# A four-layer graph network: the last add moved to GpSimd, and the planner's constants and rank offsets set anew

## The chip, the cores and the metric

The kernel runs on one core of a Trainium2 chip. The metric is the device time of one execution in microseconds; the lower the better. The core has a matmul engine (TensorE, "PE" in the profile), a vector engine (VectorE, "DVE"), an activation engine (ScalarE, "ACT"), GpSimd ("POOL"), and SyncE ("SP"), which here does nothing but issue DMA transfers.

## The reference, cut to what matters

The input is `x`, 128 graphs of 128 nodes with 256 features, and `adj`, a 128x128 matrix of zeros and ones for each graph. Four layers follow each other; each normalizes `x`, applies relu, and adds the result of a graph layer to `x`.

```python
A = (adj != 0)
# layer 0: three steps of a gated recurrent cell
h = relu(layernorm(x)); h0 = h
for i in range(3):
    m = h @ weight[i]
    aggr = einsum('bst,bsd->btd', A, m)
    h = gru_cell(aggr, h)        # r, z, n from aggr @ w_ih.T and h @ w_hh.T
x = x + h
# layer 1: sums over neighbours, by relation (adj holds only 0 and 1 here)
h = relu(layernorm(x)); x = x + (einsum(adj == 1, h) @ w1 + b1)
# layers 2 and 3: attention over neighbours
h = relu(layernorm(x)); Wh = h @ W.T
e = leaky_relu(Wh @ a1 + (Wh @ a2).T); e = where(adj, e, -inf)
x = x + softmax(e) @ Wh
```

The change touches the line `x = x + h` of layer 0, and the order in which everything is issued.

## The kernel before, in words

The 128 graphs are worked on in 32 groups of four (`G = 4`), so one tile has 128 partitions and 4 x 128 = 512 columns. Up to five groups are open at once (`AHEAD = 5`), in different layers. For the gates and for two of the layers' weights an operand is split into three parts in a rounded format (`F32R`): `forms` writes `hi` (L955 on ACT or L957 on DVE), `lo` (L961 on DVE) and their difference (L470, on POOL in nearly all cases), and PE makes three passes for each product (L992).

**One group.** `load` brings `x` and `adj`. `norm` computes the statistics on DVE (L696 and the small instructions up to L720), the power -0.5 on POOL (L722), and the scaled relu on ACT (L743). The recurrent cell runs three times in `step`: gathers over the neighbours (L974), the products of the gates (L992), gate functions on ACT (L1005, L1013, L1023, L1040) and DVE (L1035, L1042, L1045, L1048). The state is kept with features in the partitions. To come back to nodes in the partitions it is transposed by `turn`: DVE transposes 32x32 blocks inside a tile (L490), a transfer writes the tile to DRAM (`give`, L493, `swap<-big`), and four transfers read it back with the blocks exchanged (`take`, L502, `big<-swap`, or `wide<-swap` for the two tiles at a group's start, which are taken together). After the third step the two halves of `h` so transposed are added to `x` by `residual` (L1080), one instruction of 128x512 for each half; `x` is fetched a second time for this (`x1_`, L513). In the last two groups PE transposes instead and DVE adds straight from PSUM (L1073). Then come layer 1 (`neighbours`, with `bias` on POOL at L756) and two attention layers (`attention`, `attend`; L1119 computes two dot products per graph on DVE). The matmul of a layer with its neighbours is L765, with its weights L819 or L775. The attention's rows go through DRAM as well (`line<-small`, `big<-line`).

**The order.** Nothing is issued in program order. Every piece of work is recorded as an `Op` with its engine or engines, its planned length, what it reads and writes, and a `late` for the time from its end until its result may be read by another engine. `Plan.order` then simulates the engines with these planned times and writes out one order for all of them; each engine executes its own part of it strictly in sequence and waits by semaphores. The rank of an operation is its group times `PERIOD` (`CLOSE` for the last groups), minus the length of the longest way from it to its group's end, plus an offset from the table `OFFSETS`, which has an entry for each stage and each place in the code. The stages stand three times in the table: 0 to 7 for most groups, 10 to 17 for the last four, 20 to 27 for the first. On each engine the operation of lowest rank among those that can start is placed; an operation that could start only over `NEAR` ns later stands back. `SOON` is the margin by which an operation with two possible engines goes to its second.

**Planned times of transfers.** An operation on SP has the issue time as its length (`dma`, 470 ns; four times that for a `take`), and its result may be read by an engine `e` after `late + LAG["SP"] + HOP[e]`, that is `late` + 4500 + 40 ns for DVE or ACT, or after `late + OWN["SP"]` by another transfer of SP. `late` is `GIVE`, `TAKE`, `LINE` or `SPREAD` for the transfers of `turn` and `attend`, and 0 for the others. So a `take` has 4 x 470 + 2040 ns in the plan before.

**The add in question.** It is recorded with two engines, `(dve(T), 1250)` ns on DVE and POOL, and `port=True`: the plan lets no two operations with that mark run at the same time on DVE and POOL.

A branch on the largest entry of `adj` chooses between two programs; with these inputs the one described here runs.

Of the kernel before, what the change touches and what calls it, by code (L numbers as in the profile page):

```python
# [18 lines left out]
P = 128  # L19
# [19 lines left out]
OWN = {"PE": 0, "ACT": 125, "DVE": 125, "POOL": 80, "SP": 2500, "ACTQ": 2500}  # L39
PERIOD = 29902  # L40
CLOSE = 7183
CLOSING = 2
SOON = -210
# [3 lines left out]
LINE, SPREAD = 0, -1000  # L47
GIVE = -400
TAKE = -2500
TENSOR = ()  # L50
BLOCK = 32
NEAR = 69
# [24 lines left out]
def act(n, ptrs=0):  # L77
    return 50 + 95 * ptrs + 0.833 * n


def dve(n):
    return 68 + n / 0.96


def dma(kb):
    return 470
# [3 lines left out]
    0: (-70252, -12514, 2287, 8809, -26238, -146194, 10750, 55634, 30994, -54821, -2879, -215, -254,),  # L90
    1: (-77596, -18751, -40109, -33244, -13055, -53723, -68528, 1773, -34806, -135119, 879, -98768, 51856,
        44795, -64452, -2716,),
    2: (-95804, -20611, 70568, -66959, -6282, -38365, 6331, 7167, -87557, -120685, 144159, 0, -60172, 22200,
        253, 2907, 38047,),
    3: (-102445, -23990, 38859, 16506, -38395, -77755, 61821, 576, 58832, 37279, 38392, 48590, -137270, -161,
        -4329, 88294, -5659, -1511, -24936, -35483,),
    4: (9420, 6970, 96990, 45577, 14137, -3081, -28597, -108133, -850, -77398, -8748, -81, 24213, -39147,
        5274, -117520, -39070, 4328, 73461, 2677, -9322, 38218,),
    5: (-53063, -10484, 13614, 9709, -9223, 0, 86360, -49387, 3891, -79089, 22834, -12125, 42, -143071,
        -20815, -7001, 39402, 8197, 210921, 979, -8129, 55104, -109511, 178418, -171023, -17919, -45955,  # L100
        32785, 202299, 15929, -75290, -16189,),
    6: (-8401, 1876, 0, -2867, -17545, -54409, -177384, 6635, -4173, 16809, 64025, 1422, -41374, 3498, 7298,
        112681, -960, 0, -167733, 3047, -20901, 48681, -50794, 104147, -14530,),
    7: (2011, -43268, -7473, -2193, -13120, 17374, 10030, 24727, -8835, -59753, 29500, -32772, -10542,
        -85496, -6214, -47593, 4322, -5746, -43839, -101654, -3101, 9392, -18883,),
    10: (31340, 140410, 166041, 86764, 86271, -82403, 47762, 173067, 157481, -33091, 90840, -8460, 85813,),
    11: (-90811, -5747, -11338, -10756, 2168, -27498, -36330, -9110, 13623, -65824, 59954, -36485, 65854,
        102114, -39462, 10659,),
    12: (-88894, -2718, 120398, -47746, 16864, -33143, 17060, 25017, -58235, -111482, 170409, 89873, -65258,
        61044, 3422, 23111, 49690,),  # L110
    13: (-59071, 17894, 109447, 41927, -4268, -51312, 111328, 77067, 108356, 88471, 46360, 263340, -35253,
        23414, 79162, 211888, 10834, -10383, 74698, 67176,),
    14: (-32758, 12684, 122607, -43352, -20519, -34186, -56784, -88737, -18648, -122741, -24236, -29303,
        31876, -49287, -17477, -128202, -71886, 71670, 64769, 11212, -103569, -34527,),
    15: (-186417, -106904, -40789, -64266, -8033, -13445, 16411, -115394, -129609, -221523, -34547, -153159,
        -40482, -146129, -99541, -93701, -50044, 14115, 99121, -155460, -34394, 49772, -135635, 90451,
        -238640, -50117, -75732, -67304, 110359, -120923, -153053, -106347,),
    16: (90192, 31519, 28924, 59971, 13927, -108659, -126696, 35607, 7022, 44259, 134646, 83504, 72967,
        -71833, 139898, 214088, -4475, 66727, -178916, 46932, 84371, 67621, 13000, 119832, 93548,),
    17: (2011, -43268, -7473, -2193, -13120, 17374, 10030, 24727, -8835, -59753, 29500, -32772, -10542,  # L120
        -85496, -6214, -47593, 4322, -5746, -43839, -101654, -3101, 9392, -18883,),
    20: (-107741, -75380, -118420, -44708, -69924, -229335, -95079, 10513, -7484, 27055, -96949, -215, -254,),
    21: (-241039, -37443, -85617, -204164, -130954, -212658, -180409, -165567, -39823, -261311, -133885,
        -103620, -20641, -66103, -225402, -138454,),
    22: (-120431, -90137, 129948, -127092, 11177, -90000, -80347, -35815, -106293, -139261, 141530, -54256,
        -129233, 7860, -119111, 29072, 3576,),
    23: (-144176, -87227, -85789, 1378, -81324, -238467, -3162, -78700, 46997, -3871, 33809, 42358, -177604,
        -35904, -119077, -63937, -38348, -135903, -24936, -35483,),
    24: (-200969, -199448, -70412, -199813, -160146, -250664, -235592, -342997, -205357, -303708, -186137,
        -202706, -168399, -243146, -236370, -300082, -270699, -214705, -104544, 2677, -9322, 38218,),  # L130
    25: (-61251, -50204, -55609, -84828, -90010, 10545, -51986, -177143, -111208, -144284, 59013, -46623,
        -56779, -179794, -83802, -190091, -64080, -63359, 54466, -41363, -72589, -54011, -140205, 135055,
        -306980, -77123, -140787, 32785, 202299, 15929, -75290, -16189,),
    26: (-81589, -13318, 8156, -109205, -83353, -110277, -231535, -35494, -89897, 10694, 20288, -77730,
        -166910, -72981, -43136, 895, -48027, -102602, -242066, -114463, -91143, 43689, -72571, 104147,
        -14530,),
    27: (2011, -43268, -7473, -2193, -13120, 17374, 10030, 24727, -8835, -59753, 29500, -32772, -10542,
        -85496, -6214, -47593, 4322, -5746, -43839, -101654, -3101, 9392, -18883,),
# [235 lines left out]
def kernel(  # L374
# [49 lines left out]
    def build(general):  # L424
# [53 lines left out]
        def turn(nm, srcs, dst=None, w=None):  # L478
# [7 lines left out]
            for k, (src, r) in enumerate(srcs):  # L486
                part = chunk(f"part{nm}{k}")

                def within(src=src, part=part):
                    nc.vector.transpose(part.t, src())  # L490

                def give(k=k, part=part):
                    nc.sync.dma_start(out=swap.t[k * G : (k + 1) * G].rearrange("g p c -> p g c"),  # L493
                                      in_=part.t.rearrange("p (g c) -> p g c", g=G))

                op("DVE", dve(T) + 15, within, r=[r], w=[part])
                op("SP", 470, give, r=[part], w=[(swap, {k})], late=GIVE)

# [6 lines left out]
            op("SP", 470 * P // BLOCK, take, r=[swap], w=[w], late=TAKE)  # L505
# [3 lines left out]

        def fetch(gi, name, after=()):  # L510
            xt = Buf(xs, f"{name}{gi}")
            for g2 in range(G // 2):
                op("SP", dma(256), lambda g2=g2: nc.sync.dma_start(  # L513
                    out=xt.t[:, 2 * g2 : 2 * g2 + 2, :],
                    in_=x[ds(gi * G + 2 * g2, 2)].rearrange("g n d -> n g d")),
                   w=[(xt, {2 * g2, 2 * g2 + 1})], after=after)
            return xt
# [4 lines left out]
        def again(gi, after):  # L522
            ai = Buf(adjs, f"again{gi}")
            op("SP", dma(256), lambda: nc.sync.dma_start(
                out=ai.t.rearrange("p (g j) -> p g j", g=G),
                in_=adj[ds(gi * G, G)].rearrange("g i j -> i g j")), w=[ai], after=after)
            return ai

        def load(gi):
            xt, ai = fetch(gi, "x0_"), Buf(adjs, f"adj{gi}")  # L530
            op("SP", dma(256), lambda: nc.sync.dma_start(
                out=ai.t.rearrange("p (g j) -> p g j", g=G),
                in_=adj[ds(gi * G, G)].rearrange("g i j -> i g j")), w=[ai])
            state[gi] = xt, ai
# [383 lines left out]
        def group(gi):  # L918
# [21 lines left out]
            def step(i, hs, hT):  # L940
# [136 lines left out]
                for k, h in enumerate(hs_new if i == L - 1 else ()):  # L1077
                    def residual(eng, k=k, h=h):
                        part = xt.t[:, :, k * P : (k + 1) * P]
                        (nc.gpsimd if eng == "POOL" else nc.vector).tensor_tensor(  # L1080
                            part, part, h.t.rearrange("p (g d) -> p g d", g=G), ALU.add)

                    op(("DVE", "POOL"), (dve(T), 1250), residual, r=[h], w=[(xt, set(range(G)))], port=True)
# [3 lines left out]
            for i in range(L):  # L1087
# [7 lines left out]
            op("SP", dma(256), lambda: nc.sync.dma_start(  # L1095
                out=aiT.t.rearrange("p (g j) -> p g j", g=G),
                in_=adjT[ds(gi * G, G)].rearrange("g i j -> i g j")), w=[aiT], after=late)
# [12 lines left out]
            def attention(i, mask):  # L1110
# [4 lines left out]
                for g in range(G):  # L1115
# [9 lines left out]
                    op("DVE", 850, terms, r=[(hs[g // 2], {g}), ub[i]], w=[junk, (s, {("ei", g)})], port=True)  # L1125
# [159 lines left out]
```

## Time and profile before

| what | us |
|---|---|
| median of 3 runs | 2353.08 |
| lowest and highest run | 2349.69, 2353.46 |
| profiled execution | 2353.06 |
| its span in the profile | 2351.2 |
| PE busy | 2291.9 (97%) |
| DVE busy | 1978.2 (84%) |
| ACT busy | 1582.0 (67%) |
| POOL busy | 912.4 (39%) |
| L1080 on DVE, 47 times | 40.9 |
| L1080 on POOL, 13 times | 17.1 |

The profile is of one execution. The span goes from the first to the last instruction; the profiled execution's own time is 1.86 us longer. TensorE's granted clock was 0.996 of its full speed. Busy times of PE include the modelled ends of pipelined matmuls. A line number is that of the kernel before. "<-" in a row of waits stands between who waited and for whom; a letter q after an engine's name is its queue.

### The profile page before, as it was taken

Reading aid. Unit: us, or ns where it says so; the run is one execution under the profiler, and the core shown is the slowest. Engines: PE = TensorE matmul, PEld = TensorE weight load, DVE = VectorE, ACT = ScalarE, POOL = GpSimd, SP = SyncE. Lnnn points to the kernel's source line nnn. Section 1 sums busy time; section 2 is a strip of 40 time slices with the busy share of each in tenths; the row PEclk is TensorE's granted clock in tenths of the full one; section 3 lists DMA queues with packets and bytes.
Section 4 is the critical chain, followed back from the end, with each engine's and each line's share of the span. In section 5 each row is a group of like instructions: output and inputs, shape, how many; then the busy total and the mean of one; then the engine's idle time right before and its main releaser. Section 6 shows DMA issues by size and latency. Waiting matters only on the chain.

```text
span 2351.2 us, 39064 instructions
## 1 busy us (share of the span) xinstructions
PE 2291.9 (97%) x12137; PEld 1947.2 (83%) x12137; DVE 1978.2 (84%) x5405; ACT 1582.0 (67%) x3272; POOL 912.4 (39%) x729
## 2 busy tenths in 40 slices
PE   7999999999999999999999999999999999999997
PEld 6788888888888888888888888888888888788885
DVE  7858888888888888888888888888888888888887
ACT  6566676766676666666666766666766666666665
POOL 2334334443334443334343334343334343344421
PEclk9999999999999999999999999999999999999999
DMA  8535445555445455455455455455554555545431
GB/s 249 143 83 110 96 90 124 117 128 116 102 110 125 111 133 113 100 117 117 114 126 118 107 115 115 114 129 116 108 115 112 118 122 109 128 103 118 105 77 43
DMA packets 951273, 270.36 MB, mean 115 GB/s; under 512 B 677008, under 2 KB 939280, under 8 KB 951056
## 3 DMA queue, kind: packets, MB, share of 16 engines
q1 hardware_dynamic: 949968, 266.72, 50.0%
q8 instruction: 99, 1.62, 0.3%
q14 instruction: 118, 0.97, 0.2%
q10 hardware_dynamic: 1088, 1.05, 0.1%
HBM read 168.96 MB, written 98.69 MB: 114 GB/s over the span
## 4 chain that ended last, share of the span: by engine, by line
PE 64%; DVE 14%; DMA 10%; ACT 6%; SPq 4%; issue 3%; DVEq 0%; POOL 0%; ACTq 0%
PE bank L992 40%; PE bank L819 7%; PE bank L765 6%; PE bank L974 5%; PE bank L775 5%; DMA swap<-big 4%; SPq L502 4%; DMA big<-swap 3%; DVE junk L1119 3%; DVE form L961 2%; DMA wide<-swap 2%; ACT big L743 1%; DVE wide L1042 1%; DVE wide L1045 1%; DVE big L490 1%
## 5 line engine op out<-in xcount | busy, mean ns | idle before, releaser
L992 PE MATMUL bank<-form,wh_s 128*128 128x512 f32 x3456 | 953.4, 396 | 8.7 <-ACT bank L1005 4.6
L992 PE MATMUL bank<-form,wi_s 128*128 128x512 f32 x3456 | 944.0, 393 | 1.6 <-ACT bank L1013 0.9
L470 POOL TENSOR_TENSOR form<-form,form 128x512 fp32r<-128x512 f32 x383 | 517.7, 1362 | 800.4 <-DVE form L961 565.0
L992 PEld LDWEIGHTS bank<-form,wi_s 128*128 128x128 f32 x3456 | 644.1, 188 | 143.6 <-ACT bank L1013 3.1
L992 PEld LDWEIGHTS bank<-form,wh_s 128*128 128x128 f32 x3456 | 631.8, 188 | 151.5 <-ACT bank L1005 15.8
L1013 ACT ACTIVATE bank<-bank 128x512 f32<-128x512 f32 x448 | 255.4, 574 | 325.7 <-PE bank L992 324.4
L722 POOL TENSOR_TENSOR small<-small,nhalf 128x4 f32<-128x4 f32 (+2 forms) x140 | 142.2, 1020 | 408.8 <-DVE small L720 338.9
L1119 DVE CUSTOM_DVE_ANT_0 junk<-big,ub 128x256 bf16<-128x256 f32 x512 | 244.5, 478 | 14.2 <-ACT big L743 0.5
L743 ACT ACTIVATE big<-xs,small 128x256 f32<-128x256 f32 x384 | 200.1, 590 | 21.6 <-DVE small L726 12.2
L696 DVE BATCH_NORM_STATS2 small<-xs 128x6 f32<-128x256 f32 x512 | 190.0, 415 | 7.3 <-DMA xs<-in_x_dram 6.0
L470 POOL TENSOR_TENSOR cform<-cform,cform 128x512 fp32r<-128x512 f32 x120 | 155.2, 1294 | 96.2 <-DVE cform L811 83.0
L490 DVE STREAM_TRANSPOSE big<-wide 128x512 f32<-128x512 f32 x252 | 173.1, 697 | 4.0 <-ACT wide L743 2.3
L1035 DVE SCALAR_TENSOR_TENSOR bank<-big,bank 128x512 f32<-128x512 f32 x192 | 131.9, 690 | 48.5 <-PE bank L992 35.9
L955 ACT ACTIVATE form<-wide 128x512 fp32r<-128x512 f32 x179 | 109.2, 626 | 83.7 <-DMA wide<-swap 43.4
L1179 ACT ACTIVATE big<-big,small 128x128 f32<-128x128 f32 x256 | 99.8, 392 | 70.0 <-DVE small L1173 69.7
L1023 ACT ACTIVATE bank<-bank,b_rz 128x512 f32<-128x512 f32 x192 | 123.4, 655 | 34.0 <-PE bank L992 30.1
L1210 DVE SCALAR_TENSOR_TENSOR xs<-bank,small,xs 128x256 f32<-128x256 f32 x256 | 118.4, 475 | 31.6 <-PE bank L775 23.0
L1042 DVE TENSOR_TENSOR wide<-wide,bank 128x512 f32<-128x512 f32 x192 | 126.9, 682 | 21.4 <-ACT bank L1040 21.1
L765 PE MATMUL bank<-big,big 128*128 128x128 f32 x1024 | 130.7, 277 | 11.9 <-DVE wide L1045 7.1
L1023 ACT ACTIVATE big<-bank,b_rz 128x512 f32<-128x512 f32 x192 | 130.1, 681 | 16.3 <-PE bank L992 12.1
L765 PEld LDWEIGHTS bank<-big,big 128*128 128x128 f32 x1024 | 123.1, 192 | 19.4 <-DVE wide L1045 9.9
L974 PE MATMUL bank<-adjs,big 128*128 128x128 f32 x1024 | 131.2, 276 | 6.4 <-DMA big<-swap 5.1
(105 smaller groups left out, 3297.5 us busy)
## 6 DMA issues: line engine op xcount, KB each, us to landing
swap<-big SPq DMA_DIRECT2D x312, 256.0 KB, 2.5
big<-swap SPq DMA_DIRECT2D x992, 64.0 KB, 2.3
xs<-in_x_dram SPq DMA_DIRECT2D x128, 256.0 KB, 3.1
adjs<-in_adj_dram SPq DMA_DIRECT2D x64, 256.0 KB, 3.4
wide<-swap SPq DMA_DIRECT2D x128, 128.0 KB, 3.6
big<-line SPq DMA_DIRECT2D x60, 256.0 KB, 3.9
out_dram<-xs SPq DMA_DIRECT2D x30, 512.0 KB, 3.1
big<-in_adj_dram SPq DMA_DIRECT2D x32, 256.0 KB, 4.0
```

Of the source, the lines that this page charges most:

```text
L470: (nc.gpsimd if eng == "POOL" else nc.vector).tensor_tensor(at(df), at(lo).bitcast(F32), at(hi).bitcast(F32), ALU.subtract)
L490: nc.vector.transpose(part.t, src())
L696: op("DVE", dve(D), lambda g=g: nc.vector.bn_stats(s.t[:, ST + 6 * g : ST + 6 * g + 6], xt.t[:, g, :]), r=[(xt, {g})], w=[(s, {("mv", g)})])
L743: nc.scalar.activation(place(g), xt.t[:, g, :].rearrange("p (k m) -> p k m", k=KC), AF.Relu, bias=s.t[:, MR + g : MR + g + 1], scale=s.t[: ...
L765: nc.tensor.matmul(ps.t[:, (len(gs) * k + j) * P : (len(gs) * k + j + 1) * P], hs[g // 2].t[:, (g % 2) * D + k * P : (g % 2) * D + (k + 1) ...
L819: nc.tensor.matmul(po.t[:, j * D : (j + 1) * D], fs[f].t[:, (len(gs) * k + j) * P : (len(gs) * k + j + 1) * P], w.t[:, f, k, :], start=(st ...
L974: nc.tensor.matmul(pg.t[:, g * P : (g + 1) * P], of()[:, g * P : (g + 1) * P], flags(m0)[:, g * P : (g + 1) * P], start=True, stop=True,)
L992: nc.tensor.matmul(ps.t, w.t[(slice(None), *row, j, k, slice(c * P, (c + 1) * P))], b.t, start=(start and x == 0), stop=(x == len(terms) - ...
L1013: nc.scalar.mul(ps.t, ps.t, by)
L1023: op("ACT", act(T, 1), lambda: nc.scalar.activation(to.t, ps.t, AF.Tanh, bias=b_rz.t[:, c : c + 1], scale=0.5), r=[b_rz, *([ps] if kept el ...
L1042: op("DVE", dve(T), lambda c=c, ps=ps: nc.vector.tensor_tensor(hT.t[:, c, :], hT.t[:, c, :], ps.t, ALU.subtract), r=[ps], w=[(hT, {c})])
L1119: nc.vector.tensor_tensor_reduce(out=junk.t, in0=part, in1=ub[i].t[:, v, :], op0=ALU.mult, op1=ALU.add, scale=1.0, scalar=0.0, accum_out=s ...
```

## The change

It does four things. The last add of layer 0 is recorded for POOL alone, with the same planned 1250 ns. The planner's constants are set to other values: the issue of a transfer is 530 ns in place of 470, ACT and DVE instructions are 7 and 6 ns longer, the two dot products of L1119 880 ns in place of 850, and `SP`'s own wait, `GIVE`, `TAKE`, `LINE` and `SPREAD` are changed together; a `take` of two tiles is planned 800 ns later than a `take` of one. `PERIOD`, `CLOSE`, `SOON` and `NEAR` have other values. All of `OFFSETS` is replaced. The loads of `x` and `adj` go through one function, `arrive`, which could issue them on ACT's queue; `QUEUE` is `"SP"`, so they stay on SP.

```diff
-OWN = {"PE": 0, "ACT": 125, "DVE": 125, "POOL": 80, "SP": 2500, "ACTQ": 2500}
-PERIOD = 29902
-CLOSE = 7183
+OWN = {"PE": 0, "ACT": 125, "DVE": 125, "POOL": 80, "SP": 4500, "ACTQ": 2500}
+PERIOD = 38729
+CLOSE = 7557
 CLOSING = 2
-SOON = -210
+SOON = 150
...
-LINE, SPREAD = 0, -1000
-GIVE = -400
-TAKE = -2500
+LINE, SPREAD = -1800, -1400
+GIVE = -2500
+TAKE = -2600
 TENSOR = ()
+ISSUE = 530
+LANDING = 4400
+QUEUE = "SP"
 BLOCK = 32
-NEAR = 69
+NEAR = 107
...
 def act(n, ptrs=0):
-    return 50 + 95 * ptrs + 0.833 * n
+    return 57 + 95 * ptrs + 0.833 * n
 def dve(n):
-    return 68 + n / 0.96
+    return 74 + n / 0.96
 def dma(kb):
-    return 470
+    return ISSUE
...
-    0: (-70252, -12514, 2287, 8809, -26238, -146194, 10750, 55634, 30994, -54821, -2879, -215, -254,),
...
+    0: (-5321, -5695, -109, -70772, 23739, 48173, -7620, -1243, 67145, 52391, 57086, -37063,),
...
-                op("SP", 470, give, r=[part], w=[(swap, {k})], late=GIVE)
+                op("SP", ISSUE, give, r=[part], w=[(swap, {k})], late=GIVE)
...
-            op("SP", 470 * P // BLOCK, take, r=[swap], w=[w], late=TAKE)
+            op("SP", ISSUE * P // BLOCK, take, r=[swap], w=[w], late=TAKE + 800 * (n - 1))
...
+        def arrive(dst, src, w, after=()):
+            on_act = QUEUE == "ACT"
+            op(QUEUE, dma(256), lambda: (nc.scalar if on_act else nc.sync).dma_start(out=dst(), in_=src), w=w,
+               after=after, late=LANDING if on_act else 0)
...
                 for k, h in enumerate(hs_new if i == L - 1 else ()):
-                    def residual(eng, k=k, h=h):
+                    def residual(k=k, h=h):
                         part = xt.t[:, :, k * P : (k + 1) * P]
-                        (nc.gpsimd if eng == "POOL" else nc.vector).tensor_tensor(
-                            part, part, h.t.rearrange("p (g d) -> p g d", g=G), ALU.add)
+                        nc.gpsimd.tensor_tensor(part, part, h.t.rearrange("p (g d) -> p g d", g=G), ALU.add)
-                    op(("DVE", "POOL"), (dve(T), 1250), residual, r=[h], w=[(xt, set(range(G)))], port=True)
+                    op("POOL", 1250, residual, r=[h], w=[(xt, set(range(G)))], port=True)
...
-                    op("DVE", 850, terms, r=[(hs[g // 2], {g}), ub[i]], w=[junk, (s, {("ei", g)})], port=True)
+                    op("DVE", 880, terms, r=[(hs[g // 2], {g}), ub[i]], w=[junk, (s, {("ei", g)})], port=True)
```

## The prediction

> **What bounds the kernel now.** I read the page's engine totals first, then PE's busy time in three stretches (the first three groups, the steady part, the last two groups), then what PE, VectorE (DVE) and ScalarE (ACT) waited for, and last the rows of the instructions that the change touches. From the page:
>
> ```profile
> span 2351.2 us, 39064 instructions
> PE 2291.9 (97%) x12137; PEld 1947.2 (83%) x12137; DVE 1978.2 (84%) x5405; ACT 1582.0 (67%) x3272; POOL 912.4 (39%) x729
> ```
>
> TensorE (PE) is busy for all but 59.3 us. No instruction of PE changes in the diff, so the change can act only on those 59.3 us and on small gaps that the modelled matmul ends hide. The three stretches (columns: PE, its weight loads, DVE, ACT, POOL) say where they lie:
>
> ```profile
> 0.00:225.00 225.00, 206.92 (x992) 170.88 (x993) 165.96 (x372) 142.81 (x294) 76.15 (x66) 0.98 0.57 145
> 225.00:2200.00 1975.00, 1953.64 (x10430) 1665.97 (x10429) 1688.95 (x4550) 1346.92 (x2757) 790.66 (x618) 1.00 0.51 115
> 2200.00:2351.20 151.20, 131.37 (x720) 110.35 (x719) 123.34 (x485) 92.24 (x223) 45.56 (x46) 0.97 0.30 71
> ```
>
> PE idles 18.1 us in the head, 21.4 us in the steady part (1.1% of it) and 19.8 us in the tail. DVE is at 86% in the steady part: near enough to PE that its delays can reach PE. PE's waits in the steady part (us in total, times, longest):
>
> ```profile
> PE bank L765 <- DVE wide L1045: 7.1, 12, 1.5
> PE bank L992 <- ACT bank L1005: 4.6, 7, 1.0
> PE bank L765 <- DMA big<-swap: 3.4, 4, 1.6
> PE bank L974 <- DMA big<-swap: 1.4, 3, 0.7
> PE bank L992 <- DVE form L961: 0.8, 3, 0.4
> PE bank L992 <- DVE form L957: 0.6, 1, 0.6
> ```
>
> Of these 17.9 us, 13.3 us are put down to DVE or to the transposing transfers, 4.6 us to ACT. No wait is long: this is the residue of a planned order whose planned times differ a little from the real ones.
>
> **The residual add.** The planner gave the last add (L1080) to DVE 47 times and to GpSimd (POOL) 13 times. The rows of these two forms, and of a DVE form that shares the port with POOL (busy, mean ns, then idle before it):
>
> ```profile
> L1119 DVE CUSTOM_DVE_ANT_0 junk<-big,ub 128x256 bf16<-128x256 f32 x512 | 244.5, 478 | 14.2 <-ACT big L743 0.5
> ...
> L1080 DVE TENSOR_TENSOR xs<-xs,big 128x512 f32<-128x512 f32 x47 | 40.9, 870 | 69.6 <-DMA big<-swap 66.5 <-issue 3.1
> L1080 POOL TENSOR_TENSOR xs<-xs,big 128x512 f32<-128x512 f32 x13 | 17.1, 1315 | 25.0 <-DMA big<-swap 21.1 <-ACT big L1179 2.8 <-DVE form L961 1.0
> ```
>
> On DVE the 47 adds cost 40.9 us of work, and DVE stood in front of them for another 69.6 us, nearly all for a transfer. Moved to POOL that is 110.5 us off DVE, 4.7% of the span; POOL gains 47 x 1.315 = 61.8 us and goes from 912 to 974 us, 41%. DVE has 13.3 us at most to give back to PE (above), so I do not count 110 us but a part of 13.3. Against it: on POOL each add takes 1315 - 870 = 445 ns longer, so 47 x 0.445 = 20.9 us of latency is added to the chain transfer, add, statistics (L696), POOL power (L722), scale (L743), matmul L765. Work of other groups, up to five open at once, covers it; if all that cover were gone the cost would be 20.9 us. The new wait also stands in POOL's queue: what is queued behind it are the splits of L470 (whose readers are PE's third passes, with PE's weight loads waiting for POOL only 1.4 us in the whole trace) and L722, for which DVE's L726 already waits 56.1 us. If POOL waits as long as DVE did, 66.5 / 45 = 1.5 us an add, that is 70 us of its 1439 us of idle time.
>
> The port between DVE and POOL shows in this stretch of the timeline (start, length):
>
> ```profile
> 963.41 1.41 POOL L470 TENSOR_TENSOR form<-form,form 128x512 fp32r<-128x512 f32 x1 [9.77 <-DVE form L961]
> ...
> 963.71 1.39 DVE L1119 CUSTOM_DVE_ANT_0 junk<-big,ub 128x256 bf16<-128x256 f32 x1
> ```
>
> That DVE instruction takes 0.42 us when POOL is quiet. Its mean of 478 ns against 420 is 58 ns x 512 = 30 us of stretching under the 503 splits, 66 biases and 13 adds of POOL (582 instructions), so 47 more by the same share are 2.4 us; the end on the other side is one blocked DVE instruction of up to 1.3 us behind each add, 61 us. I take the small end, since the planner marks both sides as users of the port and sets them apart, as it did for the 582. Even the large end is below the 110.5 us that DVE gives up.
>
> The Trainium skill, page "SBUF — State Buffer", section "Who interferes with whom", speaks against this move: a DVE instruction with two SBUF inputs and a GpSimd instruction that reads SBUF exclude each other, and the later one blocks fully. The row at 963.71 agrees (1.39 us in place of 0.42). By the rule alone the sum would take the 61 us end for DVE and little would be gained; by the rows it takes 2.4 us.
>
> **Issue times and landings.** The planner had 470 ns for one DMA issue and now has 530. Four issues of one transfer on SP, and the wait that followed the first of them:
>
> ```profile
> 960.89 3.72 SPq L502 DMA_DIRECT2D wide<-swap  x4
> ...
> 967.14 1.15 ACT L955 ACTIVATE form<-wide 128x512 fp32r<-128x512 f32 x2 [1.79 <-DMA wide<-swap]
> ...
> 969.92 1.91 SPq L502 DMA_DIRECT2D big<-swap  x4
> ```
>
> For the transfer into wide the old plan has 4 x 470 of issue and 4500 - 2500 + 40 until ACT may read it, 3.92 us; the trace took 967.14 - 960.89 = 6.25 us. The new plan has 4 x 530 + 4500 - 2600 + 800 + 40 = 4.86 us: it removes 40% of the error. The wait list has ACT idle 43.4 us in 27 of 32 groups for this transfer, and DVE 10.3 us. Neither reaches PE with more than the 1.4 us of L961 and L957. For the transfers into big the sum goes from 3.92 to 4 x 530 + 1940 = 4.06 us, and the give before them from 470 + 2100 to 530 + 2000: hardly changed. The new ACT and DVE constants (+7 and +6 ns) are nothing by themselves. The transfers, their queue and their sizes stay as they are: the function that now issues the loads goes to SP as before.
>
> **The order.** The rank offsets, the distance of groups in rank (29.9 to 38.7 us) and the waiting thresholds are all new, so nearly every instruction may change its place. The trace of before cannot show the new order; it bounds it. Below: the steady idle cannot fall by more than 21.4 us, and head and tail by no more than 37.9 us less the 8.3 us of waits for the first weights (L598 on wihT 6.3, w0T 2.0), which no order removes: 29.6 us. Above: an order that suits the chip worse can cost as much as the steady idle again, 21.4 us; nothing excludes it. I take a gain, because the two things that the plan of before had wrong in the trace (a transfer expected 2.3 us early, DVE put in front of late transfers) are both corrected in the direction of the trace.
>
> **The sum.** Of the 13.3 us put down to DVE and transfers I take 60%, 8 us: the waits of over half a microsecond go, the small ones stay. Of the 29.6 us in head and tail I take 5 us, a sixth, since few groups are open there and the chain of one group binds. ACT's 4.6 us stay. 13 us together: the profiled execution took 2353.06 us (span 2351.2 and 1.86 us around it), within 0.02 us of the median, so 2340 us. What is late next is PE itself.
>
> **The rivals.**
> 1. The plan comes true better: 2340 us, own range 2320 (all 13.3 us, and two thirds of 29.6) to 2348. 57%.
> 2. Nothing that can be told: two executions of this kernel differ by up to 0.16% (2349.69 to 2353.46), so 0.2%, 4.7 us, is what counts as a change. PE is 98.9% busy in the steady part, ACT's and DVE's waits were off the path, and offsets of tens of microseconds decide the order more than 60 ns an issue do. Also here: the change doing less than it says, as 13 of 60 adds were on POOL already. 2353 us, 13%.
> 3. Slower, by the add on POOL: place, the chain from the last transfer to L765; price, 20.9 us of latency plus up to 66.5 us of transfer waits that now hold POOL's queue in front of L722 and L470. For it: L722 is already awaited by DVE 56.1 us, and POOL has one queue. Against: 61% of POOL idle. It decides once over 13 of the 87.4 us (15%) reach PE; with 35% exposed it is 2340 + 30.6 = 2371 us. 20%.
> 4. Slower, by the order: a larger distance between groups ranks the older group's work higher, so PE finds less ready work of the next group when the older one waits. Price: the steady idle doubled, 2353 + 21 = 2374 us. Against: the next groups stay admitted and start whenever PE would idle in the plan. 10%.
>
> **How the numbers follow.** Likeliest case: 2340. Faster by over 0.2%: case 1, 0.57. Within 0.2%: case 2, 0.13. Slower: cases 3 and 4, 0.30. The range for 8 in 10 leaves out a tenth below 2320 and a tenth above 2372, between the two slower cases.
>
> **What would show it.** Right: L1080 on POOL alone, 60 times at about 1.3 us; DVE near 1940 us busy and without its 66.5 us wait; ACT's wait for wide down from 43.4 us to some 25; PE's steady idle near 13 us; PE's waits on DVE and big<-swap under 6 us. Wrong: PE waiting for POOL (L470) or for L743 by over 10 us, DVE's wait for L722 above 90 us (case 3); PE idle above 30 us in the steady part with waits spread over ACT and DVE (case 4); or these waits gone and the span the same, which would say that they were never PE's limit.

## The result and the profile after

The changed kernel takes 2466.11 us (median of 4 runs, 2463.03 to 2472.74) against 2351.39 us for the kernel before in the same comparison: a ratio of 1.049, interval 1.0467 to 1.0513. It is slower by 4.9%, some 115 us. The time lies far above the forecast range, and the sign was wrong. The page of after:

```profile
span 2461.2 us, 39056 instructions
PE 2313.7 (94%) x12137; PEld 1956.5 (79%) x12137; DVE 1910.6 (78%) x5294; ACT 1623.2 (66%) x3336; POOL 965.8 (39%) x776
```

PE executes the same 12137 matmuls. Its idle time rose from 59.3 to 147.5 us, 88.2 us more, and its busy time by 21.8 us; together that is the 110 us by which the span grew. The second part is for the most part the clock, as is worked out below. The busy time of PE by stretches (the same first two as shown of before):

```profile
0.00:225.00 225.00, 200.10 (x962) 166.76 (x963) 172.94 (x397) 141.45 (x292) 77.53 (x67) 0.95 0.57 146
225.00:2200.00 1975.00, 1869.73 (x9890) 1584.15 (x9889) 1517.28 (x4143) 1310.16 (x2658) 798.47 (x629) 0.99 0.48 109
```

The head lost 6.8 us; the steady part idles 105.3 us where it idled 21.4. So the loss is a steady one, some 3 us of idle time in each group. What PE waited for in the steady part, and the row of the transfers from which these waits come:

```profile
PE bank L770 <- DMA big<-swap: 53.9, 29, 3.4
PE bank L824 <- POOL cform L474: 28.7, 24, 1.9
PE bank L824 <- ACT bank L835: 11.3, 17, 1.1
PE bank L979 <- DMA big<-swap: 9.2, 12, 1.8
```

```profile
swap<-big SPq DMA_DIRECT2D x312, 256.0 KB, 3.7
```

L770 is the old L765, the matmul with the transposed scores; L824 is the old L819, its product with the layer's split weights; L474 is the old L470; L979 the gather, old L974; L1085 the add, old L1080. Two waits of once per group carry the loss, and both were small before. The `give`, whose median landing was 2.5 us on the page of before, now lands after 3.7 us.

**One group in the timeline.** The first wait, at layer 3's attention (the second of the two attention layers; the expectations below call it the third attention step), with start and length:

```profile
1277.94 0.46 SPq L516 DMA_DIRECT2D xs<-in_x_dram  x1
...
1278.44 1.70 SPq L497 DMA_DIRECT2D swap<-big  x3
...
1285.50 1.91 SPq L506 DMA_DIRECT2D big<-swap  x4
...
1289.28 2.47 PE L770 MATMUL bank<-big,big 128*128 128x128 f32 x16 [2.94 <-DMA big<-swap]
```

SP issued, from 1276.9 on, two loads of `x`, one of `adjT` and two gives of a later group; the third of the gives at 1278.44, issued at 1279.56, is the urgent one. Its `take` could start only at 1285.50, 5.9 us after it; the plan had 2.53 us. PE reached L770 2.94 us before the data. The transfer engines were busy nearly all the time until 1284 (PE, weight loads, DVE, ACT, POOL, then granted clock, DMA share, GB/s):

```profile
1278.00:1280.00 2.00, 2.00 (x20) 2.00 (x18) 1.77 (x5) 1.52 (x3) 1.33 (x2) 1.00 1.06 275
1280.00:1282.00 2.00, 2.00 (x13) 1.74 (x12) 1.06 (x2) 0.81 (x2) 1.12 (x1) 1.00 0.91 259
1282.00:1284.00 2.00, 2.00 (x10) 1.63 (x10) 1.93 (x8) 1.39 (x3) 1.30 (x1) 1.00 0.86 256
1284.00:1286.00 2.00, 2.00 (x11) 1.58 (x9) 0.26 (x2) 1.09 (x3) 1.02 (x1) 1.00 0.04 13
```

The second wait:

```profile
1250.78 1.29 POOL L1085 TENSOR_TENSOR xs<-xs,big 128x512 f32<-128x512 f32 x1 [2.56 <-DMA big<-swap]
...
1252.02 1.26 POOL L474 TENSOR_TENSOR cform<-cform,cform 128x512 fp32r<-128x512 f32 x1
...
1253.34 0.72 PE L824 MATMUL bank<-wa,cform 128*128 128x256 f32 x4 [1.15 <-POOL cform L474]
```

POOL stood 2.56 us in front of the add, waiting for a late transfer; DVE had written the input of the split behind it 2.4 us before the split began, and PE waited 1.15 us for that split. In all 24 of PE's waits for L474, the instruction just ahead of the split on POOL was an add that had waited (1.6 to 3.2 us).

**What a long wait costs beside itself.** After the wait at 1289.28 (clock in the column behind POOL):

```profile
1289.28:1290.50 1.22, 1.22 (x11) 1.22 (x11) 0.64 (x4) 0.00 (x0) 0.00 (x0) 1.00 0.00 0
1290.50:1291.70 1.20, 1.20 (x9) 1.20 (x8) 0.00 (x0) 0.58 (x1) 0.00 (x0) 0.60 0.02 7
1291.70:1293.00 1.30, 1.30 (x5) 1.01 (x4) 0.00 (x0) 0.95 (x2) 0.00 (x0) 0.50 0.00 0
```

The granted clock fell to half, for 3.4 us by the record of the clock, in which PE lost 1.7 us. In the steady part of the changed kernel this happened nine times (15.4 us in all, as time at the lowered clock times what it lacked), each within two microseconds of a gap between matmuls of 1.9 to 3.4 us, and never in that of the kernel before, whose longest gaps were under 2 us. Over the whole span the same product is 30.7 us after and 9.9 before: 20.8 us more, close to PE's 21.8. It is an upper bound of what PE lost, since PE also idles within such stretches. The Trainium skill, page "TensorE: Matmul & The Clock Gate", part 1, has PE's clock halved after an idle window of about 3.4 us and full again after a busy one; the length of the slow stretches agrees, and here a gap of 1.9 us was at times enough: of the gaps over 1.5 us in this steady part 9 of 21 were followed by one.

**Gives by what is ahead of them.** I took from both traces, for groups 3 to 27, the time from the issue of a give to the issue of its `take`, and counted the transfers (takes left out) that SP had issued in the 2.6 us before the give. At layer 3's attention the median is 2.40 us with none ahead in the kernel before (22 of 25 groups); in the changed one it is 3.92 us with three ahead (7 groups), 5.31 us with four (14 groups) and 4.66 us over all 25. Over all places where the `take` followed the give's landing at once, it is 3.0, 4.1, 3.9, 3.9 and 5.3 us for none to four ahead in the changed kernel, so the number ahead does not tell all. Three or more stood ahead in 22 of 128 such cases after and in 3 of 146 before.

The issues ahead cost twice. In the same 25 groups at layer 3, the give was issued 1.57 us (median) after DVE had its tile ready, in place of 0.03 us, since SP was still issuing the others; then it landed 4.64 us after its issue in place of 2.35 us. So of some 3.8 us, 1.5 are SP's own issue time and 2.3 the transfers ahead; in `loads_back` below, with these transfers behind, the two times are 0.03 and 2.29 us.

### The profile page after: what moved, and what is told of

It reads as the page before. It is cut to its first block, busy times and chain, and to the rows that moved or that the text cites. A ratio compares the mean times of both kernels' runs of the same rounds, so it can differ in the third digit from the quotient of the medians.

```text
span 2461.2 us, 39056 instructions
## 1 busy us (share of the span) xinstructions
PE 2313.7 (94%) x12137; PEld 1956.5 (79%) x12137; DVE 1910.6 (78%) x5294; ACT 1623.2 (66%) x3336; POOL 965.8 (39%) x776
## 5 line engine op out<-in xcount | busy, mean ns | idle before, releaser
L474 POOL TENSOR_TENSOR form<-form,form 128x512 fp32r<-128x512 f32 x383 | 515.3, 1358 | 987.0 <-DVE form L966 891.1
L1018 ACT ACTIVATE bank<-bank 128x512 f32<-128x512 f32 x475 | 276.4, 582 | 410.1 <-PE bank L997 404.5
L1122 DVE CUSTOM_DVE_ANT_0 junk<-big,ub 128x256 bf16<-128x256 f32 x512 | 223.2, 436 | 23.0 <-ACT big L748 0.7
L474 POOL TENSOR_TENSOR cform<-cform,cform 128x512 fp32r<-128x512 f32 x120 | 155.0, 1292 | 140.9 <-DVE cform L816 138.8
L770 PE MATMUL bank<-big,big 128*128 128x128 f32 x1024 | 139.0, 291 | 57.3 <-DMA big<-swap 54.8
L770 PEld LDWEIGHTS bank<-big,big 128*128 128x128 f32 x1024 | 130.5, 203 | 75.0 <-issue 51.8
L960 ACT ACTIVATE form<-bank 128x512 fp32r<-128x512 f32 x188 | 109.1, 597 | 72.3 <-PE bank L979 68.1
L824 PEld LDWEIGHTS bank<-wa,cform 128*128 128x128 f32 x720 | 96.9, 188 | 66.2 <-POOL cform L474 39.3
L824 PE MATMUL bank<-wa,cform 128*128 128x256 f32 x720 | 109.4, 288 | 40.9 <-POOL cform L474 28.7
L1028 ACT ACTIVATE big<-bank,b_rz 128x512 f32<-128x512 f32 x192 | 132.0, 688 | 24.1 <-PE bank L997 18.6
L979 PEld LDWEIGHTS bank<-adjs,big 128*128 128x128 f32 x1024 | 127.0, 192 | 19.7 <-issue 9.4
```

The costliest lines, as they stand in the source:

```text
L474: (nc.gpsimd if eng == "POOL" else nc.vector).tensor_tensor(at(df), at(lo).bitcast(F32), at(hi).bitcast(F32), ALU.subtract)
L770: nc.tensor.matmul(ps.t[:, (len(gs) * k + j) * P : (len(gs) * k + j + 1) * P], hs[g // 2].t[:, (g % 2) * D + k * P : (g % 2) * D + (k + 1) ...
L824: nc.tensor.matmul(po.t[:, j * D : (j + 1) * D], fs[f].t[:, (len(gs) * k + j) * P : (len(gs) * k + j + 1) * P], w.t[:, f, k, :], start=(st ...
L979: nc.tensor.matmul(pg.t[:, g * P : (g + 1) * P], of()[:, g * P : (g + 1) * P], flags(m0)[:, g * P : (g + 1) * P], start=True, stop=True,)
L1018: nc.scalar.mul(ps.t, ps.t, by)
L1122: nc.vector.tensor_tensor_reduce(out=junk.t, in0=part, in1=ub[i].t[:, v, :], op0=ALU.mult, op1=ALU.add, scale=1.0, scalar=0.0, accum_out=s ...
```

## The experiments

Two theories and a rival. **A**: the new order puts transfers that can wait ahead of urgent ones, and these land late. **B**: an add of the last `h` that waits on GpSimd holds up splits that stand behind it. **C**: the new order is worse in many small places. All times are ratios to the kernel before on the same chip, since chips differ (the kernel before had medians from 2342.83 to 2363.22 us in these comparisons). The changed kernel itself ran only in the comparison above; what an edit takes back is counted from its ratio there, 1.049, taken to hold on the other chips. Except where it is said, an order is not planned anew but edited, so that all else stays in its place.

**Transfers behind (loads_back).** After `plan.order`, transfers that stand just ahead of the urgent give are moved:

```diff
+    for give in of(order, "SP", (6, 16)):            # layer 3's scores
+        take = next(h for h in give.heirs if h.eng == "SP")
...
+            if o.tag in ((0, 0), (2, 16), (3, 17), (4, 17), (0, 10)) and o.end > give.end - 4500:
+                n += behind(order, o, take)          # x, adj, adjT, gives of a later group
```

> The changed kernel's order, with one edit: the 256 KB transfers that SP issues just ahead of the give of the third attention step's scores (loads of x, adj and adjT, and gives that are not urgent) are issued behind that step's take. Theory A, transfers queue behind each other: in the trace of after this give lands 4.7 us (median) after its issue with four transfers ahead of it and 2.3 us with none, and PE stands 54.8 us at L770 for it. So L770's wait falls below 12 us, and the time by 35 to 55 us, to 2410 to 2430. Theory B, the adds on GpSimd hold up the splits behind them: this place does not matter, the time stays within 10 us of 2466. Theory C, the new order is worse in many small places: a fall by 10 to 20 us at most.

Measured: 2442.59 us, ratio 1.0431 (1.0407 to 1.0455). The give was followed by its take after 2.35 us (from 4.66), as A says, and this matmul's row of waits fell from 53.9 to 13.5 us, of which at most 1.5 are still layer 3's; the rest stands at layer 2's attention, where it was 4.5. PE's steady idle fell from 105.3 to 84.4 us; but only a ratio of 0.006 came back, not the 0.015 to 0.023 expected. The wait list of this kernel says where it went:

```profile
ACT adjs L904 <- DMA adjs<-in_adjT_dram: 115.1, 25, 7.7
```

The `adjT` load had been moved as well, and ACT, whose next instruction in order converts it, stood still for 115 us (0.9 us in the changed kernel). The edit had exchanged one late transfer for another.

**Splits first (split_first).**

```diff
+    for i, o in enumerate(pool):                     # GpSimd's operations in order
+        if o.fn.__code__.co_name == "residual":
+            for goal in reversed(pool[i + 1 : i + 3]):
+                if goal.tag == (5, 21) and behind(order, o, goal):   # layer 2's split
```

> The changed kernel's order, with one edit: where an add of the last h stands on GpSimd's queue ahead of a split that the third pass of layer 2's weights (L824) needs, the split goes first (25 places). Theory A, late transfers alone: PE's waits at L824 come from elsewhere and stay, the time stays within 10 us of 2466. Theory B, the waiting add holds the split up: PE's wait at L824 for GpSimd falls from 28.7 us to below 8, and the time by 20 to 40 us, to 2426 to 2446. Theory C, many small places: under 10 us.

Measured: 2434.38 us, ratio 1.0361 (1.0319 to 1.0403): 0.013 of 0.049 came back, about 30 us, with 25 adds moved by one or two places. PE's wait for the split on GpSimd is gone from its list, and its steady idle fell to 78.0 us. Theory B holds as far as this: the add's place in the queue costs.

**Both edits (both).**

> The changed kernel's order with both edits: the transfers behind the third attention step's take, and the splits ahead of the adds. Theory A alone: as with the first edit alone, 2410 to 2430. Theories A and B each with its own place: the two gains add up to 60 to 95 us, 2371 to 2406, and PE's steady idle falls from 105 to about 30 us. Theory C: over 2430.

Measured: 2416.51 us, ratio 1.0307 (1.0289 to 1.0325). The gains add up (0.018 in place of 0.006 and 0.013), but the sum is smaller than A and B foresaw, and PE's steady idle is 64.5 us, not about 30: `adjT` is still late (118.4 us of ACT), which the next run removes.

**Both, with adjT left in place (urgent_split).** The list of what may be moved is reduced to the loads of `x` and the later group's gives:

```diff
+WAIT = {(6, 16): ((2, 16), (0, 10))}
```

> The changed kernel's order with the splits ahead of the adds, and of the transfers ahead of the third attention step's give only those moved behind its take that nobody waits for soon: the two loads of x and the two gives of a later group; the load of adjT keeps its place. The first attempt moved adjT too, and ACT then stood 115 to 118 us for it. Theory A with the adds' place: the give lands in about 2.4 us, ACT's wait for adjT is near zero, and the time falls by another 20 to 45 us against the first pair of edits, to a ratio of 1.010 to 1.022 to the kernel before. Theory C, many small places: within 10 us of the first pair of edits (ratio 1.027 to 1.035).

Measured: 2387.67 us, ratio 1.0107 (1.0083 to 1.0132). These two edits take back 0.038 of the 0.049, 78% of the loss, and leave the adds on GpSimd, the constants and the rest of the order as changed. PE's steady stretch and what is left of its waits:

```profile
225.00:2200.00 1975.00, 1931.93 (x10295) 1638.56 (x10294) 1575.79 (x4332) 1359.61 (x2765) 836.84 (x656) 1.00 0.50 113
```

```profile
PE bank L885 <- ACT bank L896: 18.1, 21, 1.3
PE bank L1040 <- DMA big<-swap: 9.6, 11, 1.5
PE bank L831 <- DMA big<-swap: 9.4, 14, 2.1
```

The wait for the scores' transfer is down from 53.9 to 9.4 us, that for GpSimd's split is gone from the list, ACT's wait for `adjT` is 0.8 us, and PE's steady idle is 43.1 us. The remaining 0.011 was not taken apart: it may be more places of the same kind or theory C.

**One more place cleared (clear).** The store of a finished group and a load of the next `adj` are moved behind layer 2's take as well.

```diff
+WAIT = {(6, 16): ((2, 16), (0, 10)), (5, 16): ((6, 22), (0, 0))}
```

> The same, and in front of the give of layer 2's scores the store of a finished group and a load of the next adj go behind that step's take as well. Theory A: the give of layer 2 falls from 3.4 to 4.0 us to below 2.6 us, L770's remaining wait goes, and the time falls by a further 8 to 25 us. Theory C: within 6 us of the run without this.

Measured: 2458.92 us, ratio 1.0408 (1.0386 to 1.0431): a miss for both theories' numbers. The give landed sooner (its take followed after 2.31 us in place of 3.88), and most of what the run before had won was lost again:

```profile
ACT form L1021 <- DMA wide<-swap: 132.0, 26, 6.9
```

```profile
SPq L577 <- DMA out_dram<-xs: 67.7, 28, 2.8
```

```profile
PE bank L885 <- ACT bank L896: 73.5, 23, 4.7
```

The load of `x` that comes next on SP writes the tile that the store reads, so SP stood 67.7 us for the later store (11.0 in the run without this move); ACT waited 132.0 us for the transfer into `wide` (75.6), and PE 73.5 us for ACT (18.1). The lowered clock, 20 times in the steady part, took up to another 41.0 us (3.4). That the first wait led to the others is read from these rows and was not tested. Such a wait need not cost so much: in the kernel before SP stood 69.9 us for stores, with ACT's wait for `wide` at 43.4 us. What can wait on one queue is not free to go anywhere on it.

**Added transfers, ahead and behind (burst_ahead, burst_behind).** The kernel before, with three transfers that nobody reads, once ahead of the give and once behind its take:

```diff
+    def burst():
+        for t in spare:                              # three DRAM tiles of 256 KB
+            nc.sync.dma_start(out=t, in_=tiles["wa_1"][0])
...
+                if o.tag == (6, 16):                 # burst_behind: after o.issue(), o.tag == (6, 17)
+                    burst()
                 o.issue()
```

> The kernel before with its own order, and three added transfers of 256 KB (a constant tile to spare DRAM, read by nobody) on SP ahead of each give of the third attention step's scores. Theory A, a give waits in the transfer engines for what was issued ahead: the give lands 2 to 3 us later, PE waits at L765 by up to that in each of 24 to 28 groups, 30 to 70 us slower. Theory C, only the whole order counts: the added 3 x 0.9 us of transfers have room (half of the engines' time is idle), within 8 us.

> The same three added transfers for each group, issued behind that step's take. The bytes and the issues are the same as in the run with the transfers ahead. Theory A: nothing urgent stands behind them, within 12 us of the kernel before, so that ahead and behind differ by at least 20 us. Theory of bandwidth alone, that more bytes cost wherever they are: as slow as ahead.

Measured: ahead 2383.56 us, ratio 1.0093 (1.0069 to 1.0116); behind 2366.81 us, 1.0012 (0.9997 to 1.0026). The same bytes, issued by the same engine, cost 0.9% in front of the urgent transfer and nothing that can be told behind it. In the kernel with the transfers ahead:

```profile
PE bank L765 <- DMA big<-swap: 32.0, 25, 3.0
```

Behind, the same row reads 2.1 us in 3 waits. So transfers ahead of an urgent one cost time in a kernel that has neither the new add nor the new constants, and bytes alone do not. The size was overestimated (20 us, not 30 to 70): the give landed 3.20 us (median) after its issue, 0.85 us later than in the kernel before and not 2 to 3. More came from SP itself: the give was issued 1.43 us after its tile was ready (0.03 before), behind the three issues. The expectation's mechanism, a wait in the transfer engines, is here the smaller part.

**The add's engine (adds_pool, adds_dve).** The kernel before with its 47 DVE adds on GpSimd, and the changed kernel with its 60 adds on DVE, each at its place in the order:

```diff
     issue, cut = plan.order(pools, big, verdict)
+    for o in issue:                                  # adds_pool
+        if o.fn.__code__.co_name == "residual":
+            o.eng = "POOL"
...
-                        nc.gpsimd.tensor_tensor(part, part, h.t.rearrange("p (g d) -> p g d", g=G), ALU.add)
+                        nc.vector.tensor_tensor(part, part, h.t.rearrange("p (g d) -> p g d", g=G), ALU.add)
```

> The kernel before with its own order, place by place, and one edit: the 47 adds that stood on DVE are executed by GpSimd at the same places in the order. Theory B, an add that waits on GpSimd holds up splits: slower by 15 to 50 us, with PE waits for L470 of more than 10 us. Theory A, what costs is late transfers and not the engine of the add: within 10 us of 2351, with DVE's wait of 66.5 us moved to GpSimd.

> The changed kernel's order, place by place, and one edit: all 60 adds are executed by DVE at the places in the order where GpSimd had them. Theory B, the adds on GpSimd hold up the splits behind them: PE's wait at L824 for GpSimd falls from 28.7 us to below 8 and the time by 20 to 40 us, a ratio of 1.032 to 1.041. Theory A alone, late transfers: the wait moves to DVE (over 50 us before the add), DVE stands in PE's way in its place, and the ratio stays within 1.043 to 1.055.

Measured: adds_pool 2357.82 us, ratio 1.0058 (1.004 to 1.0075); adds_dve 2472.63 us, ratio 1.0552 (1.0511 to 1.0594). Moving the add to GpSimd costs 0.6% (14 us) by itself in an order not made for it, just under what B foresaw, but not in B's way: no matmul waits for L470 there. The rows that grew are these (0.3 and 7.1 us in the kernel before):

```profile
DVE small L696 <- POOL xs L1080: 76.8, 25, 4.4
```

```profile
PE bank L765 <- DVE wide L1045: 20.5, 22, 1.9
```

The statistics (L696) read what the add writes. DVE, rid of its wait for the transfer, stood as long for GpSimd's add, and PE's wait for DVE grew. Giving the add back to DVE does not mend the changed kernel, against B's number: DVE then stood 43.1 us in front of the add, and PE's wait changed its name:

```profile
PE bank L824 <- DVE cform L816: 34.7, 24, 2.3
```

In 23 of these 24 waits an add that had waited 1.2 to 2.5 us stood four instructions ahead of L816 on DVE. So in the changed order B is true of the place in the queue and false of the engine: on either engine, the add that waits for a late transfer holds up what stands behind it.

**The constants alone (times_new).** The kernel before, planned anew with the new issue time, landings and ACT and DVE lengths, its offsets kept.

```diff
-OWN = {"PE": 0, "ACT": 125, "DVE": 125, "POOL": 80, "SP": 2500, "ACTQ": 2500}
+OWN = {"PE": 0, "ACT": 125, "DVE": 125, "POOL": 80, "SP": 4500, "ACTQ": 2500}
...
-LINE, SPREAD = 0, -1000
-GIVE = -400
-TAKE = -2500
+LINE, SPREAD = -1800, -1400
+GIVE = -2500
+TAKE = -2600
```

> The kernel before with the new issue, landing, ACT and DVE constants alone; rank offsets, distances and the choice of engine for the add as before, the order planned anew. The forecast's theory, planned times closer to the trace make the plan come true better: no slower than 2351, ACT's wait for the transfer into wide falls from 43 to about 25 us. The rival: the offsets suit only the constants with which they were searched; with others the order falls apart whatever the constants' truth, 1.01 to 1.04 times the kernel before, its PE waits in places that are neither of the two found in the changed kernel.

Measured: 2384.0 us, ratio 1.0174 (1.0148 to 1.0199). Its stretches:

```profile
0.00:225.00 225.00, 177.53 (x807) 143.13 (x808) 143.95 (x330) 119.67 (x249) 58.53 (x52) 0.91 0.49 130
225.00:2200.00 1975.00, 1954.08 (x10474) 1671.39 (x10473) 1674.04 (x4519) 1360.82 (x2750) 796.29 (x620) 1.00 0.51 115
```

The steady part idles 20.9 us, as before (21.4). The loss is in the head (47.5 us idle in place of 18.1); that the head's offsets suit only the old constants, as the rival had it, was not tested further. ACT's wait for `wide` fell to 20.6 us. So the forecast's theory missed the time, and the rival met it; the constants are no part of the steady idle time.

**The choice given back, planned anew (add_choice).** The changed kernel with the two-engine `op` of the kernel before for the add (its lines as removed in the diff above).

> The changed kernel with the planner's choice of DVE or GpSimd for the add given back, all else as changed, the order planned anew: ten adds go to DVE. If the add on GpSimd alone were the cause: a ratio below 1.02. If transfers queued ahead of gives are the larger part, or the offsets suit only the plan with which they were searched: 1.03 to 1.06, with PE's wait at L770 for the take still over 30 us.

Measured: 2470.67 us, ratio 1.053 (1.0492 to 1.0569), with 56.7 us of PE's wait at L770 over the whole span (54.8 in the changed kernel). The add alone was not the cause.

**A plan that counts the queue (queue_planned).** The changed kernel, adds on GpSimd and new constants included. In the planner, each transfer holds the engines for a time, and the landing follows from when they are free; the offsets, `PERIOD`, `CLOSE` and `SOON` were searched anew with that.

```diff
+            if eng in ("SP", "ACTQ"):
+                pipe = max(pipe, end - (0.75 * o.ns if o.most_ else 100)) + o.load
+                o.land = max(pipe, end) + DOWN
...
-                h.ready = max(h.ready, o.end + seen(o, h))
+                h.ready = max(h.ready, o.land + HOP[h.eng] if o.land else o.end + seen(o, h))
```

> The changed kernel (adds on GpSimd alone, the new constants) with a planner that counts what the transfer engines still have to do: each transfer holds them for a time read from the traces (0.89 us for 256 KB in rows of 512 bytes, 1.63 for a take of one tile, 3.26 for a take of two, 1.7 for a store), and its reader may start 1.61 us after its share is done. Rank offsets and distances searched anew with that. If the cause of the loss is the order that plans with constant landings led to, and neither the add on GpSimd nor the new issue times: the give of the third step's scores lands in under 2.8 us, PE's steady idle is below 30 us and the ratio to the kernel before 0.990 to 1.008. If the adds on GpSimd or the constants cost by themselves: 1.02 or more.

Measured: 2349.75 us, ratio 1.0006 (0.9994 to 1.0018). All of the loss is gone, with the adds on GpSimd and the new constants kept, so neither must cost. Its stretches and its gives:

```profile
0.00:225.00 225.00, 196.64 (x940) 164.18 (x941) 167.07 (x385) 135.99 (x281) 73.77 (x63) 0.96 0.57 144
225.00:2200.00 1975.00, 1962.74 (x10510) 1672.69 (x10509) 1684.49 (x4482) 1375.20 (x2795) 833.42 (x656) 1.00 0.51 116
```

```profile
swap<-big SPq DMA_DIRECT2D x312, 256.0 KB, 2.6
```

At layer 3's attention the give lands after 2.30 us (median). The steady idle is 12.3 us, less than the 21.4 of the kernel before; the head gives this back (28.4 us idle in place of 18.1), the tail idles 19.8 us as before. This run changed the plan's model and the searched numbers together, so it does not say which of the two mended the order.

**The kernel before with offsets chosen by such a model (queue_chosen).** Only the numbers of `OFFSETS` and `NEAR` differ from the kernel before.

> The kernel before (choice of engine for the add, old constants, constant landings in the plan) with offsets searched further, each order being judged by running it through a model with the transfer engines' queue and landings 0.2 us earlier and later. Theory A: an order that leaves urgent transfers free is a little better than before, a ratio of 0.988 to 0.999. Theory C or a model that misses what counts: 1.000 to 1.015.

Measured: 2353.25 us, ratio 1.0028 (1.0013 to 1.0043): slightly slower, outside theory A's range and inside the other's. The steady idle was 19.7 us; the planner still had constant landings, and a choice among its orders did not help.

No version beat the kernel before by more than its interval. queue_planned is equal to it: what its steady part won, its head gave back.

## Why the prediction was wrong, point by point

**The term that failed: the order.** The prediction bounded a worse order at the steady idle doubled, 21.4 us, and took a gain since two things that the plan of before had wrong were corrected "in the direction of the trace". The steady idle rose by 83.9 us, four times that bound, and the clock took up to 15.4 us of the steady part on top, a cost that the prediction did not count. The bound had no ground: idle time that a good order leaves says nothing of what another order costs. What stood in its place were transfers that could wait, issued ahead of the give of layer 3's scores (PE's row of waits for the `take` is 53.9 us, 49.1 of it at layer 3), and splits behind a waiting add (28.7 us). The plan sees one landing time whatever is ahead in the queue; the trace of before shows landings of 2.3 to 5.2 us for gives of one size, and the prediction set only the plan's two values for a give beside each other ("hardly changed"). That spread was the row to read.

**The constants: right and worth nothing in the steady part.** The plan of before did expect the transfer into `wide` too early. With the new constants alone ACT's wait for it fell from 43.4 to 20.6 us (some 25 were forecast), and PE's steady idle stayed at 20.9 us. In the changed kernel the same wait rose to 66.8 us; in `queue_planned`, with the same constants and another order, the row is 3.7 us. So the rise belongs to the order.

**The add: right in its numbers, wrong in its weight.** L1085 ran 60 times on POOL at 1298 ns; DVE's busy time went down to 1910.6 us. But the 110.5 us that the prediction took off DVE did not come free: with the add moved alone (`adds_pool`), DVE stood 76.8 us for the add on POOL in place of 66.5 us for the transfer, and the move cost 14 us. (In the changed order this wait is 6.5 us.) The third case (the add waits on POOL in front of L470) named the mechanism of the second wait, with PE waiting for L474 28.7 us, over the 10 us that would show it. I weighed it against 61% of idle time on POOL and 1.4 us of PE's weight loads waiting for POOL: that was a property of the order, which the change replaced. And the engine is not the point: on DVE the wait is as long (34.7 us).

**The port.** In `adds_pool`, with the same order and 47 more adds on POOL, L1119's busy time is 244.6 us in place of 244.5, so the 2.4 us taken for the port were nearly no cost, and the end of 61 us was far off. In the changed kernel the mean of L1122, the old L1119, even fell from 478 to 436 ns.

**The third and fourth case's prices.** The third case took 35% of 87.4 us, 30.6 us, as exposed. PE's wait for the split is close to that, 28.7 us, in part by luck, since the add moved alone made no such wait; the larger part of the loss came from a place that no case named. The fourth case's sign, steady idle above 30 us with waits spread over ACT and DVE, did not appear: the idle time is there, but most of it stands for a named transfer and a named split. Whether the larger distance between groups helped to make this order was not tested alone.

What stays open: why the search of offsets preferred this order. Worked out with the planner that each kernel carries, its plan leaves PE idle 2.8 us between 225 and 2200 us before and 1.5 us after, where the chip had 21.4 and 105.3; and PE's matmul with layer 3's scores is planned 1.2 us (median) after its operand may be read before, 0.3 us after. So by its own measure the new order was no worse, only tighter. That constant landings made the search go wrong is not shown: the kernel before was planned with constant landings too, `queue_planned` changed model and search together, and `queue_chosen`, where the model only chose among orders with constant landings, gained nothing.

## What to carry to other kernels

How late an urgent transfer comes depends on what was issued ahead of it, by the issue time on its queue and by what the transfer engines still have to move; a planner with fixed landings does not see the second part, and may put transfers that can wait in front of one that PE stands for. When a change replaces an order as a whole, nothing in the trace of before bounds what the new one costs: look for what its cost model leaves out, and widen the range upward. And when moving work back in a queue, ask for each moved piece who is next to wait for it: two of the edits here (`loads_back` and `clear`) mended one wait and made another.

## What the runs showed of the hardware that I had not expected

Three transfers of 256 KB issued just ahead of an urgent one cost 0.9%, some 20 us in 27 groups; behind it they cost 0.1%, within the interval, though the transfer engines' share of the steady part is 0.54 in both. With the queue full the engines moved 256 to 275 GB/s (the rows at 1278 to 1284), so 256 KB hold them for about 1 us, an estimate from these rows. In the steady part of the changed kernel a gap of 1.9 to 3.4 us between matmuls was followed in 9 of 17 cases by some 3.4 us at half the clock: a wait of 3 us then costs nearly 5, by estimate. SP, about to issue a load into a tile that a store was still reading, stood for the store's landing, 67.7 us in `clear` and 69.9 us in the kernel before, and what was next in its order stood with it.
